# A mixture-of-experts kernel on one core: where TensorE takes the transposes of outputs and of the next rows

## The chip, the core and the metric

The kernel runs on one core of a Trainium2 chip. TensorE (PE) multiplies and transposes, VectorE (DVE) and ScalarE (ACT) compute on tiles, GpSimd (POOL) and SyncE (SP) mainly issue DMAs here. The metric is the device time of one launch in microseconds, the median of the runs of a kernel. Each engine takes its own instructions in the order in which they stand in the program; semaphores make them wait for each other.

## What is computed

`x` is (4, 1024, 1024) in float32. First a cross attention adds to every token a softmax over its normalized similarities with 1024 context vectors. Then follows a mixture of experts, which takes nearly all of the time:

```python
router_probs = jax.nn.softmax(x_flat @ gate_w, axis=-1)
topk_w, topk_idx = jax.lax.top_k(router_probs, 2)          # of 8 experts
topk_w = topk_w / jnp.sum(topk_w, axis=-1, keepdims=True)
...
h = jax.lax.ragged_dot(x_rep_sort, w1, group_sizes)         # 1024 -> 3584
h = jax.nn.silu(h) * jax.lax.ragged_dot(x_rep_sort, w3, group_sizes)
out_sort = jax.lax.ragged_dot(h, w2, group_sizes)           # 3584 -> 1024
...
out = jnp.einsum('tkd,tk->td', out_rep, topk_w)
```

The layer's input is the normalized token, and `out` is added to the token.

## The kernel before

**Before the experts.** The first 550 us compute the attention and the routing, write the tokens to the output and their normalized rows to `h_d`, and fill a table of slots: for each expert, which tokens it has and with which weight.

**Runs and blocks.** The experts' work is a loop over runs on the chip (L841). A run is one expert with up to three blocks of `width` tokens (176 matmul columns for half of a block of 352); a switch picks the code for the number of blocks and the width (L845, `RUNS`). In the profiled execution there are 8 runs of 3 blocks, 24 blocks in all, with half widths of 164, 168, 176 and 180. TensorE's instructions stand in the order in which the code names them (`manual_schedule(engines={ENG.PE})`, L846); the other engines' orders are made by the framework's scheduler from the dependencies.

**A block**, `run` (L745), has two stages. Products are made by a scheme of seven products in place of eight (p1 to p7, Strassen and Winograd's): VectorE makes sums of each weight tile (`weight_sums`, L580, four instructions L585 to L588) and of the tokens (`token_factors`, L709), PE multiplies, and `combine` (L610) puts the results together from four PSUM banks.
- Stage one, i2 = 0 to 13: a tile of w1 and one of w3, each 1 MB in float32, for each of them 28 products in 56 PE instructions (L776), then silu and the product of both, into `g`.
- Stage two, quarters q = 0 to 3 of the output's columns: four tiles of w2, of 8, 8, 6 and 6 slices (`W2K`), that is 4, 4, 3 and 3 values of i2, each of which is a pair of chunks: 7 products in 14 PE instructions (L815). Then `combine` makes `y`, the quarter's result, still transposed. `y` is a single buffer.

**What is transposed.** A finished `y` has to be turned so that tokens lie in the partitions: `tokens_out` (L721) takes 3 groups, each of two 128-wide transposes on PE (L726) into a PSUM tile of the pool `pst`, and VectorE multiplies by the token's weight and adds to `acc` (L728), which holds the tokens' values gathered from the output. After the last quarter GpSimd scatters `acc` back (L733). The rows of the next block, gathered from `h_d` by GpSimd (L650), have to be turned the other way: `tokens_in` (L693) takes 6 groups of four transposes (L699) into `pst`, evicted to `x` by ScalarE (L707, even groups) and VectorE (L705, odd groups) in turn. `pst` has two buffers for both kinds. After the rows, `token_factors` makes the next block's factors, or, in a run's last block, `weight_sums` the sums of the next run's first tile, `w1a`.

**Where they stand.** The list `late` holds what is to be transposed. In stage two it is emptied in one go after the first weight tile of a quarter (L822), so the outputs of quarter q stand after the first tile of quarter q + 1; those of the last quarter stand in the next block's stage one after the first w1 tile (L784), or, between runs, after the next run's first tile (`leftover`, L742, through `y1` and `ids1`). `tokens_in` stands right after the second quarter (L831).

**Weights.** SyncE loads the weight tiles into three buffers (`wp`, L553), each as soon as PE has done with the tile three before.

Of the kernel before, what the change touches and what calls it, by code (L numbers as in the profile page):

```python
# [9 lines left out]
F32 = mybir.dt.float32  # L10
# [8 lines left out]
P = 128  # L19
N = 512  # L20
# [13 lines left out]
def kernel(  # L34
# [14 lines left out]
    nc = tc.nc  # L49
# [4 lines left out]
    KD = D // P  # L54
# [10 lines left out]
    DQ = 4  # L65
# [15 lines left out]
    ident = const.tile([P, P], F32, name="ident")  # L81
# [9 lines left out]
    with ExitStack() as st:  # L91
# [67 lines left out]
        for c in range(KC):  # L159
            pt = ps_t.tile([P, 4, P], F32, tag="pt", name="pt_w")  # L160
# [367 lines left out]
    with ExitStack() as st:  # L528
# [6 lines left out]
        pst = st.enter_context(tc.tile_pool(name="pst", bufs=2, space=PSUM))  # L535
# [5 lines left out]
        RT = 3  # L541
        HK = KD // 2
# [37 lines left out]
        def weight_sums(t, kn, halves, s=None):  # L580
            if s is None:
                s = wp.tile([P, 3, HK, P], F32, tag="s", name="ws")
            f = factors(t, kn, halves, s)
            a11, a12, a21, a22 = f["p1"], f["p2"], f["p7"], f["p4"]
            nc.vector.tensor_tensor(f["p5"], a21, a22, ALU.add)  # L585
            nc.vector.tensor_tensor(f["p6"], f["p5"], a11, ALU.subtract)  # L586
            nc.vector.tensor_tensor(f["p3"], a12, f["p6"], ALU.subtract)  # L587
            nc.vector.tensor_tensor(a21, a11, a21, ALU.subtract)  # L588
            return f
# [70 lines left out]
        rows = [fst.tile([P, D], F32, name=f"rows{s}") for s in range(RT)]  # L660
# [31 lines left out]

        def tokens_in():  # L693

            for s in range(RT):
                for h in range(2):
                    pt = pst.tile([P, N], F32, tag="pt", name="pt_h")
                    for k in range(HK):
                        nc.tensor.transpose(  # L699
                            pt[:, ts(k, P)], rows[s][:, ts(HK * h + k, P)], ident  # L700
                        )
                    src = pt.rearrange("p (a b) -> p a b", b=P)
                    dst = x[:, ds(HK * h, HK), ts(s, P)]
                    if h % 2:
                        nc.vector.tensor_copy(dst, src)  # L705
                    else:
                        nc.scalar.copy(dst, src)  # L707

        def token_factors(n):  # L709

# [8 lines left out]
            return dict(p1=b11, p2=b21, p3=b22, p4=t4, p5=t1, p6=t2, p7=t3)  # L719

        def tokens_out(ids, split, q, y):  # L721
            yv = y.rearrange("p (d c) -> p d c", d=2)
            for s, r in enumerate(split):
                pt = pst.tile([P, N], F32, tag="pt", name="pt_y")
                for d in range(2):
                    nc.tensor.transpose(pt[:r, ts(d, P)], yv[:, d, ds(s * P, r)], ident)  # L726
                part = acc[s][:r, ts(q, QW)]
                nc.vector.scalar_tensor_tensor(  # L728
                    part, pt[:r, :QW], ids.bitcast(F32)[:r, s, 1:2], part, ALU.mult, ALU.add
                )  # L730
            if q == DQ - 1:
                for s, r in enumerate(split):
                    nc.gpsimd.indirect_dma_start(  # L733
                        out=of,
                        out_offset=bass.IndirectOffsetOnAxis(ap=ids[:r, s, 0:1], axis=0),
                        in_=acc[s][:r, :],
                        in_offset=None,
                        bounds_check=T - 1,
                        oob_is_err=False,
                    )  # L740

        def leftover():  # L742
            tokens_out(ids1, [P] * RT, DQ - 1, y1)

        def run(i, ex, s0, blocks, width):  # L745
            n = width // 2
            split = [min(P, width - c) for c in range(0, width, P)]

            def take_ids():
                ids = ip.tile([P, RT, IDW], I32, tag="ids", name="ids")  # L750
                nc.vector.tensor_copy(ids, ids0)
                rd = ip.tile([P, RT], I32, tag="rd", name="rd")
                nc.vector.tensor_copy(rd, rd0)
                return ids, rd

            late = [leftover]
            right = token_factors(n)
            for b in range(blocks):
                ids, rd = take_ids()
                last = b == blocks - 1  # L760
                if not last:
                    load_rows(s0 + (b + 1) * width)
                g = hp.tile([P, NI, 7, n], F32, tag="g", name="g")
                for i2 in range(NI):
                    cs = []
                    for wf, wa, tag in ((w1f, w1a, "c1"), (w3f, w3a, "c3")):
                        t = load(wf, ex, 0, KD, i2 * QW) if b or i2 else wa
                        if t is w1a:
                            left = factors(w1a, KD, False, s1a)
                        else:  # L770
                            left = weight_sums(t, KD, False)
                        pp = banks()
                        for p in ORDER if b or i2 else EARLY:
                            bk, half = BANK[p]
                            for k in range(HK):
                                nc.tensor.matmul(  # L776
                                    pp[bk][:, ts(half, n)], left[p][:, k, :],
                                    right[p][:, k, :],
                                    start=(k == 0), stop=(k == HK - 1),
                                )  # L780
                        c = gp.tile([P, 4 * n], F32, tag=tag, name=tag)
                        combine(pp, n, c, 2 * n)
                        cs.append(c)
                        while late:  # L784
                            late.pop(0)()
                    c1, c3 = cs
                    nc.scalar.activation(c1, c1, AF.Silu)  # L787
                    nc.vector.tensor_tensor(
                        g[:, i2, B11 : B22 + 1, :].rearrange("p a b -> p (a b)"), c1, c3,
                        ALU.mult,  # L790
                    )
                    token_sums(g[:, i2, :, :], n)

                if last:
                    load_first(i + 1)
                    beyond = ip.tile([P, RT], F32, tag="beyond", name="beyond")
                    nc.vector.tensor_scalar(
                        beyond, at, float(width), float(NONE), ALU.is_ge, ALU.mult
                    )
                    nc.vector.tensor_tensor(ids1[:, :, 0], beyond, ids[:, :, 0], ALU.add)  # L800
                    nc.vector.tensor_copy(ids1[:, :, 1], ids[:, :, 1])
                for s, r in enumerate(split):
                    gather(acc[s][:r, :], of, rd, s, r)
                for q in range(DQ):
                    pp = banks()
                    i2 = 0
                    for kn in W2K:
                        t = load(w2f, ex, 2 * i2, kn, q * QW)
                        left = weight_sums(t, kn, True)
                        for k in range(kn // 2):  # L810
                            for p in ORDER:
                                bk, half = BANK[p]


                                nc.tensor.matmul(  # L815
                                    pp[bk][:, ts(half, n)], left[p][:, k, :],
                                    g[:, i2, RIGHT[p], :],
                                    start=(i2 == 0 and half == 0),
                                    stop=(i2 == NI - 1 and p in ENDS),
                                )  # L820
                            i2 += 1
                        while late:  # L822
                            late.pop(0)()
                    if last and q == DQ - 1:
                        combine(pp, n, y1, XW)
                        break
                    y = gp.tile([P, 2 * XW], F32, tag="y", name="y", bufs=1)
                    combine(pp, n, y, XW)
                    late.append(lambda a=ids, d=q, e=y: tokens_out(a, split, d, e))
                    if q == 1:  # L830
                        tokens_in()  # L831
                        if last:
                            weight_sums(w1a, KD, False, s1a)
                        else:
                            right = token_factors(n)

        load_first(0)
        tokens_in()
        weight_sums(w1a, KD, False, s1a)
        n_run = nc.values_load(run_n, min_val=1, max_val=NRUN)  # L840
        with tc.For_i(0, n_run) as i:  # L841
# [3 lines left out]
            for k in tc.Switch(kind, len(RUNS)):  # L845
                with tc.manual_schedule(engines={ENG.PE}):  # L846
                    run(i, ex, s0, *RUNS[k])
        leftover()


# [26 lines left out]
```

## Time and profile before

| | us |
|---|---|
| median of 3 runs | 9158.44 (9154.5 to 9159.08) |
| the profiled execution's own time | 9149.25 |
| its span, first to last instruction | 9147.6 |
| before the loop over runs | about 550 |
| one block, stage one and two (width 352) | about 361 |

The profile is of one execution. Busy time of PE is the union of its matmuls' durations, which overlap, since they are pipelined; PEld are the weight loads, which run beside them. A line such as `L726 PE MATMUL pt_y<-ident,y` names the line of the kernel, the engine, the operation, and what it writes and reads. The largest groups are the products:

```profile
L776 PE MATMUL ps<-x,wt 128*128 128x168 f32 (+3 forms) x15744 | 2510.5, 309 | 0.0
L815 PE MATMUL ps<-g,wt 128*128 128x168 f32 (+3 forms) x10752 | 2027.1, 309 | 0.0
```

After the bar stand the busy time in us and the mean duration of one in ns, then the idle time just before. In a timeline, each row is a start, a duration and what ran, merged where instructions follow each other, with the idle time before it and its cause in brackets.

### The profile page before, as it was taken

To read this page: it belongs to the slowest core of one execution; us is meant where nothing else is said; L and a number is where in the kernel's file an instruction comes from. 1 tells how busy PE (TensorE), PEld (TensorE's weight loads), DVE (VectorE), ACT (ScalarE), POOL (GpSimd) and SP (SyncE) were. 2 spreads that over 40 slices of the span, in tenths; PEclk is the share of its full clock that TensorE was granted. 3 is DMA by queue.
4 is the path that set the end of the run, shared out by engine and by line. 5 is a ranking of instruction groups with operands and counts; after the bars stand their busy time and mean duration, and the time that the engine had idled before them with its cause. 6 is when DMAs were issued, how large, how long until landed. Compare 5 with 4: busy or idle time off the path is not lost. (4 is left out here: it accounts for less than half of the span.)

```text
span 9147.6 us, 139985 instructions
## 1 busy us (share of the span) xinstructions
PE 8852.5 (97%) x59458; PEld 8654.2 (95%) x59459; DVE 5120.9 (56%) x10062; ACT 697.9 (8%) x1527; POOL 409.4 (4%) x503
## 2 busy tenths in 40 slices
PE   8969999999999999999999999999999999999999
PEld 5569999999999999999999999999999999999999
DVE  5655655655645555556546556465565565555554
ACT  3310000000000000000000000000000000000000
POOL 2310000000000000000000000000000000000000
PEclk9979999999999999999999999999999999999999
DMA  3234444443433434344434434434443444434343
GB/s 132 110 120 140 142 143 142 137 146 129 158 128 120 143 130 140 127 139 137 142 129 144 140 119 141 141 129 148 141 147 127 131 137 133 139 129 140 125 137 124
DMA packets 1117374, 1236.39 MB, mean 135 GB/s; under 512 B 35552, under 2 KB 1077984, under 8 KB 1116576
## 3 DMA queue, kind: packets, MB, share of 16 engines
q1 hardware_dynamic: 1079424, 1114.54, 37.2%
q0 software_dynamic: 32656, 107.24, 3.3%
q8 instruction: 501, 8.21, 0.4%
q10 hardware_dynamic: 4496, 3.97, 0.1%
q14 instruction: 297, 2.43, 0.1%
HBM read 1155.26 MB, written 73.53 MB: 134 GB/s over the span
## 5 line engine op out<-in xcount | busy, mean ns | idle before, releaser
L776 PE MATMUL ps<-x,wt 128*128 128x168 f32 (+3 forms) x15744 | 2510.5, 309 | 0.0
L776 PEld LDWEIGHTS ps<-x,wt 128*128 128x128 f32 x15744 | 2353.5, 190 | 0.0
L815 PE MATMUL ps<-g,wt 128*128 128x168 f32 (+3 forms) x10752 | 2027.1, 309 | 0.0
L585 DVE TENSOR_TENSOR ws<-wt 128x512 f32<-128x512 f32 (+1 forms) x1040 | 693.0, 666 | 2077.1 <-DMA wt<-in_L_ffn_w_dram 2021.0
L815 PEld LDWEIGHTS ps<-g,wt 128*128 128x128 f32 x10752 | 1688.8, 190 | 0.0
L776 PE MATMUL ps<-xs,ws 128*128 128x168 f32 (+3 forms) x10624 | 1659.2, 309 | 0.0
L815 PE MATMUL ps<-g,ws 128*128 128x168 f32 (+3 forms) x8064 | 1615.4, 309 | 0.0
L776 PEld LDWEIGHTS ps<-xs,ws 128*128 128x128 f32 x10624 | 1579.1, 190 | 0.0
L815 PEld LDWEIGHTS ps<-g,ws 128*128 128x128 f32 x8064 | 1294.7, 190 | 0.3 <-DVE y L620 0.2
L620 DVE TENSOR_TENSOR c<-ps,p1s 128x352 f32<-128x352 f32 (+3 forms) x672 | 345.9, 515 | 1103.0 <-PE ps L776 1075.0
L776 PE MATMUL ps<-x,ws 128*128 128x168 f32 (+3 forms) x5312 | 883.2, 309 | 0.0
L776 PE MATMUL ps<-xs,wt 128*128 128x168 f32 (+3 forms) x5248 | 872.6, 309 | 0.0
L776 PEld LDWEIGHTS ps<-x,ws 128*128 128x128 f32 x5312 | 804.1, 190 | 0.0
L776 PEld LDWEIGHTS ps<-xs,wt 128*128 128x128 f32 x5248 | 794.4, 190 | 0.0
L586 DVE TENSOR_TENSOR ws<-ws,wt 128x512 f32<-128x512 f32 (+1 forms) x1040 | 692.2, 666 | 30.2
L587 DVE TENSOR_TENSOR ws<-wt,ws 128x512 f32<-128x512 f32 (+1 forms) x1040 | 682.8, 657 | 0.0
L588 DVE TENSOR_TENSOR wt<-wt 128x512 f32<-128x512 f32 (+1 forms) x1040 | 682.5, 656 | 0.0
L619 ACT COPY p1s<-ps 128x168 f32<-128x168 f32 (+3 forms) x768 | 227.8, 297 | 5286.9 <-PE ps L815 2830.1
L787 ACT ACTIVATE c<-c 128x672 f32<-128x672 f32 (+3 forms) x336 | 260.9, 777 | 2559.0 <-DVE c L624 2504.9
L624 DVE TENSOR_TENSOR c<-ps,vu 128x352 f32<-128x352 f32 (+3 forms) x672 | 343.1, 511 | 84.1 <-PE ps L776 80.4
L622 DVE TENSOR_TENSOR vu<-ps,c 128x352 f32<-128x352 f32 (+3 forms) x672 | 341.5, 508 | 6.5 <-PE ps L776 6.2
L650 POOL DMA_INDIRECT rows<-h_d,rd x75 | 82.8, 1104 | 5037.6 <-issue 2487.4
(186 smaller groups left out, 3690.3 us busy)
## 6 DMA issues: line engine op xcount, KB each, us to landing
wt<-in_L_ffn_w_dram SPq DMA_DIRECT2D x848, 1024.0 KB, 4.9
wt<-in_L_ffn_w_dram SPq DMA_DIRECT2D x192, 768.0 KB, 4.6
xt<-in_x_dram SPq DMA_DIRECT2D x32, 512.0 KB, 4.4
out_dram<-x SPq DMA_DIRECT2D x32, 512.0 KB, 2.9
h_d<-hn SPq DMA_DIRECT2D x32, 512.0 KB, 2.6
w1a<-in_L_ffn_w_dram SPq DMA_DIRECT2D x9, 1024.0 KB
w3a<-in_L_ffn_w_dram SPq DMA_DIRECT2D x9, 1024.0 KB, 12.8
cx<-in_ctx_dram SPq DMA_DIRECT2D x4, 1024.0 KB, 8.1
```

Of the source, the lines that this page charges most:

```text
L585: nc.vector.tensor_tensor(f["p5"], a21, a22, ALU.add)
L586: nc.vector.tensor_tensor(f["p6"], f["p5"], a11, ALU.subtract)
L587: nc.vector.tensor_tensor(f["p3"], a12, f["p6"], ALU.subtract)
L588: nc.vector.tensor_tensor(a21, a11, a21, ALU.subtract)
L619: nc.scalar.copy(p1s, pp[0][:, :n])
L620: nc.vector.tensor_tensor(pair(c), pair(pp[1]), twice(p1s), ALU.add)
L622: nc.vector.tensor_tensor(vu, pair(pp[2]), twice(c[:, n : 2 * n]), ALU.add)
L624: nc.vector.tensor_tensor(mid, pair(pp[3]), vu, ALU.add)
L650: nc.gpsimd.indirect_dma_start(out=dst, out_offset=None, in_=src, in_offset=bass.IndirectOffsetOnAxis(ap=rd[:n, s : s + 1], axis=0),)
L776: nc.tensor.matmul(pp[bk][:, ts(half, n)], left[p][:, k, :], right[p][:, k, :], start=(k == 0), stop=(k == HK - 1),)
L787: nc.scalar.activation(c1, c1, AF.Silu)
L815: nc.tensor.matmul(pp[bk][:, ts(half, n)], left[p][:, k, :], g[:, i2, RIGHT[p], :], start=(i2 == 0 and half == 0), stop=(i2 == NI - 1 and ...
```

## The change

The transposes stay as they are, group by group. `tokens_in` and `tokens_out` no longer emit their groups, but return a list of steps, one for each group: 6 for rows, 3 for outputs; the scatter of `acc` becomes a part of its own output step. The steps go into `late`, the rows' behind the outputs of the second quarter, and behind them one step more, `sums`, for the token factors or the sums of `w1a`. From `late` one step is taken at a time: in stage one after each weight tile, in stage two after each pair of chunks but a quarter's first. So a quarter's outputs stand after its successor's pairs 2, 3 and 4; the rows stand in the third quarter after pairs 5 to 10, and `sums` after pair 11; the outputs of the last quarter stand after the first three weight tiles of what follows.

```diff
         def tokens_in():
-            for s in range(RT):
-                for h in range(2):
-                    pt = pst.tile([P, N], F32, tag="pt", name="pt_h")
...
+            def step(s, h):
+                pt = pst.tile([P, N], F32, tag="pt", name="pt_h")
...
+            return [lambda s=s, h=h: step(s, h) for s in range(RT) for h in range(2)]
...
         def tokens_out(ids, split, q, y):
             yv = y.rearrange("p (d c) -> p d c", d=2)
-            for s, r in enumerate(split):
+            def step(s, r):
                 pt = pst.tile([P, N], F32, tag="pt", name="pt_y")
...
-            if q == DQ - 1:
-                for s, r in enumerate(split):
+                if q == DQ - 1:
                     nc.gpsimd.indirect_dma_start(
...
+            return [lambda s=s, r=r: step(s, r) for s, r in enumerate(split)]
...
-            late = [leftover]
+            late = leftover()
...
                         cs.append(c)
-                        while late:
+                        if late:
                             late.pop(0)()
...
                             i2 += 1
-                        while late:
-                            late.pop(0)()
+                            if late and i2 > 1:
+                                late.pop(0)()
...
-                    late.append(lambda a=ids, d=q, e=y: tokens_out(a, split, d, e))
+                    late += tokens_out(ids, split, q, y)
                     if q == 1:
-                        tokens_in()
-                        if last:
-                            weight_sums(w1a, KD, False, s1a)
-                        else:
-                            right = token_factors(n)
+                        late += tokens_in()
+
+                        def sums():
+                            nonlocal right
+                            if last:
+                                weight_sums(w1a, KD, False, s1a)
+                            else:
+                                right = token_factors(n)
+
+                        late.append(sums)
```

More of the change, by code (lines that the diff above doesn't have):

```diff
@@ L693, in tokens_in @@
         def tokens_in():
-            for s in range(RT):
-                for h in range(2):
-                    pt = pst.tile([P, N], F32, tag="pt", name="pt_h")
[L698 to L705, printed above, removed]
-                    else:
-                        nc.scalar.copy(dst, src)
+            def step(s, h):
+                pt = pst.tile([P, N], F32, tag="pt", name="pt_h")
+                for k in range(HK):
+                    nc.tensor.transpose(
+                        pt[:, ts(k, P)], rows[s][:, ts(HK * h + k, P)], ident
+                    )
+                src = pt.rearrange("p (a b) -> p a b", b=P)
+                dst = x[:, ds(HK * h, HK), ts(s, P)]
+                if h % 2:
+                    nc.vector.tensor_copy(dst, src)
+                else:
+                    nc.scalar.copy(dst, src)
+            return [lambda s=s, h=h: step(s, h) for s in range(RT) for h in range(2)]
         def token_factors(n):
@@ L740, in tokens_out @@
                     )
+            return [lambda s=s, r=r: step(s, r) for s, r in enumerate(split)]
         def leftover():
-            tokens_out(ids1, [P] * RT, DQ - 1, y1)
+            return tokens_out(ids1, [P] * RT, DQ - 1, y1)
         def run(i, ex, s0, blocks, width):
@@ L828, in run @@
                     combine(pp, n, y, XW)
-                    late.append(lambda a=ids, d=q, e=y: tokens_out(a, split, d, e))
+                    late += tokens_out(ids, split, q, y)
                     if q == 1:
-                        tokens_in()
-                        if last:
-                            weight_sums(w1a, KD, False, s1a)
-                        else:
-                            right = token_factors(n)
+                        late += tokens_in()
[3 more added lines that the diff above has]
+                                weight_sums(w1a, KD, False, s1a)
+                            else:
+                                right = token_factors(n)
+                        late.append(sums)
         load_first(0)
-        tokens_in()
+        for step in tokens_in():
+            step()
         weight_sums(w1a, KD, False, s1a)
@@ L847 @@
                     run(i, ex, s0, *RUNS[k])
-        leftover()
+        for step in leftover():
+            step()
 _INS = [
```

## The prediction

> **What bounds the kernel now.** I read the busy table first: TensorE is in use over the whole span and no other engine is near it.
>
> ```profile
> PE 8852.5 (97%) x59458; PEld 8654.2 (95%) x59459; DVE 5120.9 (56%) x10062; ACT 697.9 (8%) x1527; POOL 409.4 (4%) x503
> ```
>
> So the time is the length of PE's own queue: what shortens that queue shortens the kernel, if nothing else then becomes late. Next, who PE waits for. Two of the four longest entries lie at the transposes that the change moves, L726 (outputs) and L699 (rows), and they are put down to the evictions of their PSUM tiles:
>
> ```profile
> PE pt_h L699 <- DMA w3a<-in_L_ffn_w_dram: 51.5, 1, 51.5
> PE pt_y L726 <- DVE acc L728: 48.2, 97, 1.9
> PE ps L776 <- issue: 36.6, 4, 10.5
> PE pt_h L699 <- ACT x L707: 30.1, 60, 0.7
> ...
> PE pt_h L699 <- DVE x L705: 2.0, 7, 0.3
> ```
>
> (us in total, times, longest.) The 51.5 us is the one wait before the loop over runs; that part isn't touched. 48.2 + 30.1 + 2.0 = 80 us, but this is a lower end: a wait counts only from the modelled end of the transpose before it (272 ns after its start), while in a steady row the next would have started after 0.11 us. So I look at start to start in the timeline, at one set of rows and one set of outputs:
>
> ```profile
> 8703.58 0.46 PE L815 MATMUL ps<-g,wt 128*128 128x176 f32 x2
> 8703.88 1.04 PE L699 MATMUL pt_h<-ident,rows 128*128 128x128 f32 x8
> 8705.15 0.66 PE L699 MATMUL pt_h<-ident,rows 128*128 128x128 f32 x4 [0.24 <-ACT x L707]
> 8706.48 1.25 PE L699 MATMUL pt_h<-ident,rows 128*128 128x128 f32 x8 [0.68 <-ACT x L707]
> 8708.41 0.66 PE L699 MATMUL pt_h<-ident,rows 128*128 128x128 f32 x4 [0.68 <-ACT x L707]
> 8708.90 0.76 PE L815 MATMUL ps<-g,wt 128*128 128x176 f32 x4
> ```
>
> ```profile
> 8681.77 0.60 PE L726 MATMUL pt_y<-ident,y 128*128 128x128 f32 x4
> 8682.19 1.48 DVE L728 SCALAR_TENSOR_TENSOR acc<-pt_y,ids,acc 128x256 f32<-128x256 f32 x3 [0.51 <-PE pt_y L726]
> 8682.73 0.17 PEld L726 LDWEIGHTS pt_y<-ident,y 128*96 128x96 f32 x2 [0.60 <-DVE acc L728]
> 8682.73 0.42 PE L726 MATMUL pt_y<-ident,y 128*96 128x128 f32 x2 [0.36 <-DVE acc L728]
> ...
> 8682.99 0.76 PE L815 MATMUL ps<-g,wt 128*128 128x176 f32 x4
> ```
>
> The first 8 row transposes take 1.04 us to their last end, so (1.04 - 0.27) / 7 = 0.11 us each; there are two PSUM buffers (pst), so the third group stands still until the first is evicted, and so on. Outputs: four go at once, the third pair waits until VectorE has evicted the first (8682.19 + 0.49).
>
> **The sum.** The trace holds 24 blocks (8 runs of three). From all start times: 24 stretches of 24 row transposes at L699, and 96 of 6 output transposes at L726. First transpose to next matmul, less 0.109 us for each transpose, leaves standing time:
> - rows: 50.7 us, 2.1 us per block;
> - outputs between the tiles of the second product (quarters 0 to 2): 72 stretches, 40.8 us, 0.57 us each;
> - outputs of quarter 3, after the next block's first w1 tile: 24 stretches, 26.2 us; mostly 0.9 us, since VectorE has the combination of that tile in front.
>
> In all 117.7 us of 9149, 4.9 us a block. The chain of waits confirms that this lies on the path: the evictions are its links between stretches of matmuls.
>
> **What the change does, part by part.** *Transposes.* Their number is the same: per block 24 + 4 x 6 = 48, at 0.109 us 5.2 us. They are a piece of PE's queue wherever they stand. What changes is that a group (2 for outputs, 4 for rows) is followed by a 14-matmul pair of chunks (14 x 0.149 = 2.09 us at width 352) or a whole tile of 56 (8.36 us). A buffer is needed again two groups later, 4.2 us at the least, where an eviction takes 0.49 to 0.68 us. All 117.7 us can go if no eviction is later than that.
>
> *More changes of kind.* Stretches of transposes per block go from 5 to 18. What does one cost? In the start times the entry is the matmul's usual pitch (8703.58, two matmuls at 0.149, 8703.88) and the exit is 0.109 plus 0.002 us. 13 more at 0.002 us, over 24 blocks: 0.6 to 0.9 us. Here a rule of the Trainium skill speaks against the change: TensorE: Matmul & The Clock Gate, Part 4: PE-mode transpose, puts a transpose at about 275 ns in a kernel's context, most of it access latency. The profile's duration, 272 ns, is the same; but the pitch is 0.109 us, since successors start under it. If each of the 13 new stretches showed that latency once (0.164 us), it would cost 13 x 0.164 x 24 = 51 us, and the gain be 66; the 120 exits in this trace show none of it, though they all come after rows of 6 or 24. I take 0.9 us. The same section says that transposes do not count as activity for the clock, which would speak for breaking up a row of 5 us; the granted clock in the window 8703 to 8710 is 1.00, so there is nothing to win here (0.80 in the window 8034 to 8060, at a change of runs, is what a throttled stretch looks like).
>
> *VectorE's order.* Evictions on VectorE stand in a fixed order behind weight sums that wait for weights. The built program shows the order of the third quarter, the tightest: sums of the third weight tile around the output evictions, then L585, L586 and L588 of the fourth tile, then the copies of the row groups (0,1) and (1,1), then the first token factor, then the next quarter's first tile with the copy of (2,1). From the quarter's start T, PE asks:
>
> - output groups after chunk pairs 2, 3, 4: T + 4.2 to T + 8.8. The third needs the first's buffer, evicted right after L585 of the third tile, which starts at T + 4.5 to 6.6 in quarters 0, 1 and 3 of this trace: evicted by about T + 7.7.
> - row groups after pairs 5 to 10, ScalarE and VectorE by turns; so the VectorE ones always take the same buffer. (1,1), after pair 8, comes at 8 x 2.09 + 3 x 0.22 + 3 x 0.44 = T + 18.7 and needs the copy of (0,1). That stands behind L585 of the fourth tile, which starts at T + 12.4 to 13.75 in every quarter of this trace. It shifts by 0.4 us, as two output groups now lie in front of the end of the first tile; so about T + 14, then 0.56 + 0.56 + 0.55 + 0.68: done near T + 16.3. Slack some 2.4 us.
> - (2,1), after pair 10, needs the copy of (1,1), written under pair 9. No weights are in front of it. It fits.
>
> Where the cover goes, PE stands still for what is missing. y has one buffer: combined by about T + 2.5, first read at T + 4.2, last at T + 8.8, written again from T + 30.
>
> *Token factors and sums of w1a* are asked for after pair 11 of the third quarter, 23 us later than before, and needed some 35 us on. The sums of w1a keep their place in VectorE's order; the factors run in the third quarter's last third, where the trace has VectorE waiting for weights. 0 us. *Scatters* (GpSimd) leave after their own output group, two tiles later for the last; read back only by the next gather, over 200 us later. 0. SP's and GpSimd's orders are unchanged; the next row gather needs the rows read, 23 us later, and has 200 us. 0.
>
> *What is late next.* With 4.9 us less per block of 360, PE asks for weights 1.4% faster. A 1 MB tile lands 4.9 us after issue, per 8.36 us tile, and the sums of the fourth tile end near T + 16 for use at about T + 26. Nothing.
>
> 9149.25 - (117.7 - 0.9) = 9032.4 us for the profiled execution; its time is 9.2 us under the median of the runs, so the median becomes 9158.44 - 116.8 = **9042 us**.
>
> **Rivals.**
> - *Part of the waits stays*, as changes of kind cost more than the long rows show, or evictions are now and then late. For: no group of 2 or 4 between dense matmuls with both edges is in this trace. Against: edges of 0.002 us. With 51 us lost, 9093; with a quarter of the waits back, 9071. Chance 0.14.
> - *Weights or another engine fill the gap*, and the time stays: VectorE is at 56% and its idle time ends on weights (2021 us in L585's row), so they could be late once PE runs ahead. Against: 8 to 10 us of slack. 9150 to 9158. Chance 0.03.
> - *Slower: PE, strictly in order, stands before the row group (1,1)* because its buffer's eviction is behind a weight sum that waits for a DMA. In the trace before, the sums ahead of an eviction always had their weights by then. It starts when the fourth tile's L585 is 2.4 us later than estimated, and outweighs the gain when it is 2.4 + 4.9 = 7.3 us later in every block, at T + 21. With 10 us late, 24 x (10 - 2.4 - 4.9) = +65: 9223. The trace has no start later than T + 13.75 in 96 quarters. Chance 0.05.
> - *The change doesn't do what it says*: the built program has the groups between the pairs on PE. No chance given.
>
> **How the numbers follow.** Likeliest 0.78: 9042, give or take 9, about what one execution and the median differ by. The low end is 9033. The high end goes into the partly hidden case, up to a quarter of the waits, 9072. A measurement here can tell about 0.2%, 18 us; so faster 0.92 (the first case and the first rival), same 0.03, slower 0.05.
>
> **What would show it.** Right: waits of L726 and L699's line in the loop (now L730) on L732, L705 and L707 nearly gone; transposes in x2 and x4 between x14 matmuls, 0.109 us pitch; PE's busy time slightly changed, span near 9032. Wrong: a wait on DVE x L705 of microseconds (the slower rival); intervals of 0.2 us or more at the edges (first rival); new waits of the products' matmuls (now L781 and L820) on weight sums (second).

## The result and the profile after

The changed kernel takes 9035.69 us (9034.8 to 9036.42), the kernel before 9158.76 us in the same series: a ratio of 0.9864, 95% interval 0.9851 to 0.9876. Predicted were 9042 us, within 9033 to 9072. The profiled execution takes 9036.42 us against 9149.25, 112.8 us less; 116.8 were predicted.

The busy table, then PE's waits (us in total, times, longest) at the lines of the transposes:

```profile
PE 8818.7 (98%) x59458; PEld 8659.7 (96%) x59459; DVE 5115.4 (57%) x10062; ACT 698.7 (8%) x1527; POOL 423.7 (5%) x503
```

```profile
PE pt_h L699 <- DMA w3a<-in_L_ffn_w_dram: 51.5, 1, 51.5
...
PE pt_y L730 <- issue: 1.3, 1, 1.3
PE pt_y L730 <- DVE acc L732: 0.8, 1, 0.8
...
PE pt_h L699 <- DVE x L705: 0.2, 1, 0.2
```

The instructions are as many as before. What is left of waits at L730 and L699 is the one before the loop and the one after it; the 48.2, 30.1 and 2.0 us are gone. PE's busy time is 33.8 us less although it does the same: each wait began under the tail of a transpose, which counted as busy.

The chain of waits of one block (start, us, what) shows the new order, which is PE's alone:

```profile
8605.80 2.09 PE ps L820 x14
8607.89 0.22 PE pt_y L730 x2
8608.11 2.09 PE ps L820 x14
8610.20 0.44 PE pt_h L699 x4
8610.64 2.09 PE ps L820 x14
8612.73 0.44 PE pt_h L699 x4
...
8622.84 0.44 PE pt_h L699 x4
8623.28 12.53 PE ps L820 x84
```

A pair of chunks is 2.09 us, an output group 2 x 0.109 us, a row group 4 x 0.109. Before, the same chain had ScalarE and VectorE as links between the transposes, as here at one set of rows:

```profile
8704.51 0.59 ACT x L707
8705.15 0.67 PE pt_h L699 x4
8705.84 0.59 ACT x L707
8706.48 1.26 PE pt_h L699 x8
```

In the timeline of the changed kernel the edges are seen start to start:

```profile
8609.74 0.46 PE L820 MATMUL ps<-g,wt 128*128 128x176 f32 x2
8610.04 0.60 PE L699 MATMUL pt_h<-ident,rows 128*128 128x128 f32 x4
8610.48 0.76 PE L820 MATMUL ps<-g,wt 128*128 128x176 f32 x4
```

Two matmuls take 0.30 us, as between matmuls alone, and four transposes 0.44. From all start times the standing time, counted as in the prediction, is 0.2 us, of 117.7.

| start to start, us, inside the loop over runs | before | after |
|---|---|---|
| first to last PE instruction | 8583.2 | 8469.0 |
| standing at transposes | 117.7 | 0.2 |
| of these: rows / outputs in stage two / in stage one | 50.7 / 40.8 / 26.2 | 0.1 / 0.1 / 0.0 |
| the seven changes of run | 75.6 | 75.7 |

(The loop here begins with the last transposes before it.) 114.2 us are gained there; the stage before it was 1.0 us longer in this execution, and the end behind PE's last instruction 0.4 us.

### The profile page after: what moved, and what is told of

The parts are those of the page before. It is cut to its first block, busy times and chain, and to the rows that moved or that the text cites. A ratio compares the mean times of both kernels' runs of the same rounds, so it can differ in the third digit from the quotient of the medians.

```text
span 9034.7 us, 139994 instructions
## 1 busy us (share of the span) xinstructions
PE 8818.7 (98%) x59458; PEld 8659.7 (96%) x59459; DVE 5115.4 (57%) x10062; ACT 698.7 (8%) x1527; POOL 423.7 (5%) x503
## 5 line engine op out<-in xcount | busy, mean ns | idle before, releaser
L820 PE MATMUL ps<-g,wt 128*128 128x168 f32 (+3 forms) x10752 | 2071.0, 309 | 0.0
L585 DVE TENSOR_TENSOR ws<-wt 128x512 f32<-128x512 f32 (+1 forms) x1040 | 693.7, 667 | 1991.4 <-DMA wt<-in_L_ffn_w_dram 1948.6
```

The lines of the kernel that those rows point to most:

```text
L820: nc.tensor.matmul(pp[bk][:, ts(half, n)], left[p][:, k, :], g[:, i2, RIGHT[p], :], start=(i2 == 0 and half == 0), stop=(i2 == NI - 1 and ...
```

## The experiments

My theory: in a row of groups, PE, strictly in order, finds both PSUM buffers of the transposes taken from the third group on and stands for an eviction, so the gain is the standing time and no more. The rivals: it is VectorE's combination ahead of the evictions, that is the place, that makes the wait; it is the number of buffers as such; or a part of the gain has another cause. (A row of groups with more than two buffers was not run.)

### The same kernel again

No edit.

> The changed kernel once more, for the size of its gain. If the gain is the standing time of PE at the transposes and nothing else (117.7 us in the trace of before, 0.2 us in that of after), the median lies 113 to 118 us under the kernel before. The first comparison of medians gave 123 us; if something else is gained too that the trace does not show as standing time, it is 120 us or more again.

9033.77 us (9027.33 to 9034.48) against 9161.15: a ratio of 0.9862 (0.9847 to 0.9877), by the medians 127 us. The profiled execution takes 9034.48 us, with 0.2 us of standing time. That is the expected sign of something more than 118 us, so I followed it below.

### One part alone: rows, or outputs

Rows one at a time, outputs in a row (`in_a_row` takes all steps of a list at once):

```diff
-            late = leftover()
+            late = [lambda: in_a_row(leftover())]
...
-                            if late and i2 > 1:
+                            if late and i2 > 3:
...
-                    late += tokens_out(ids, split, q, y)
+                    late.append(lambda o=tokens_out(ids, split, q, y): in_a_row(o))
```

> Rows one group at a time, outputs in a row after a quarter's fourth pair of chunks (the end of its first weight tile) as before. Theory (PE stands for the third and later group of a row, which finds both PSUM buffers taken): the 50.7 us at the rows go, the 66.9 us at the outputs stay: 50 us faster than before, about 9108. Rival (most is gained where VectorE has the combination in front, that is at the outputs of the last quarter, and rows in a row cost little, since ScalarE takes half of them): 20 us or less.

Outputs one at a time, rows in a row:

```diff
-                        late += tokens_in()
+                        in_a_row(tokens_in())
...
-                        late.append(sums)
+                        sums()
```

> Outputs one group at a time, rows in a row right after the second quarter as before. Theory: 66.9 us faster than before (40.8 in stage two, 26.2 in stage one), about 9092; with the rows-only kernel the two gains add up to that of the whole change. Rival (the parts overlap: once PE no longer stands at the one, VectorE is later for the other): the two gains sum to clearly more or less than 117 us, by 15 us or more.

Rows only: 9104.51 us, a ratio of 0.9942 (0.9929 to 0.9956). Outputs only: 9080.96, a ratio of 0.9915 (0.9902 to 0.9929). PE's waits, rows only, then outputs only:

```profile
PE pt_y L730 <- DVE acc L732: 51.5, 97, 2.4
...
PE pt_h L699 <- DVE x L705: 0.2, 1, 0.2
```

```profile
PE pt_h L699 <- ACT x L707: 30.1, 60, 0.7
PE pt_h L699 <- DVE x L705: 2.6, 9, 0.4
...
PE pt_y L730 <- DVE acc L732: 0.8, 1, 0.8
```

Each part takes its own wait away and leaves the other's nearly where it was: 70.4 us of standing time stay in the first (66.9 at the outputs before), 51.7 in the second (50.7 at the rows before). In the loop the profiles gain 44.0 and 65.2 us, together 109.2, the whole change 114.2. So the parts add up to within 5 us, and neither rival holds. By the medians each kernel of this series gains 12 to 15 us more than its profile does in the loop, the whole change too.

### Place without granularity

Rows in one row still, but after the third quarter's seventh pair of chunks; outputs in a row as before:

```diff
-                        late += tokens_in()
+                        late.append(lambda: in_a_row(tokens_in()))
...
-                            if late and i2 > 1:
+                            if late and i2 in (4, 7, 11):
```

(The outputs' edits are those of the rows-only kernel.)

> The place of the rows without the granularity: outputs in a row as before, rows in one row too, but after the third quarter's seventh pair of chunks in place of right before that quarter, where VectorE is busy with the combination. Theory (two buffers and a row of six groups make the wait, wherever the row stands): rows stand for 1.5 to 2.1 us per block as before, outputs as before: within 15 us of the kernel before, 9144 to 9159. Rival (the wait comes from VectorE's combination in front of the copies, so the new place is what gains): the 50 us of the rows go, about 9108.

9128.77 us, a ratio of 0.9973 (0.9962 to 0.9984): by the medians 28 us faster than before, between both expectations. The rows' standing time is 27.3 us, of 50.7. The timeline of one such row (width 328):

```profile
851.19 0.44 PE L824 MATMUL ps<-g,wt 128*128 128x164 f32 x2
851.47 1.04 PE L699 MATMUL pt_h<-ident,rows 128*128 128x128 f32 x8
852.75 2.64 PE L699 MATMUL pt_h<-ident,rows 128*128 128x128 f32 x16 [0.24 <-ACT x L707]
855.23 0.72 PE L824 MATMUL ps<-g,wt 128*128 128x164 f32 x4
```

24 x 0.109 are 2.62 us, and the row takes 3.76: 1.14 us of standing, where it was 2.1. So my theory was half right for the rows: the wait that two buffers make, when VectorE is free, is 1.14 us a block; 0.98 us more went with the old place. There VectorE has `combine` and weight sums ahead of its copies, in the row of before that the prediction shows:

```profile
8705.66 0.52 DVE L624 TENSOR_TENSOR y<-ps,vu 128x352 f32<-128x352 f32 x1
8706.10 0.33 DVE L625 TENSOR_TENSOR y<-ps,vu 128x176 f32<-128x176 f32 x1
8706.35 0.68 DVE L705 COPY x<-pt_h 128x512 f32<-128x512 f32 x1
```

The second group was transposed by 8704.9 and is copied only from 8706.35 to 8707.03. Yet the fourth group starts at 8706.48, as soon as ScalarE has copied the third (8705.84 + 0.58). So at the old place the groups do not take the two buffers in turn: the fourth uses the one that the third has just left. In the trace of before its transposes wait for ScalarE's semaphore in all 24 rows, in the kernel with the new place for VectorE's. That is why the table of waits names ScalarE for the rows although VectorE is the late one. How the 0.98 us divide between VectorE's lateness and the other order of buffers is not shown. One group at a time avoids all of it.

### How many at a time

In stage two, two steps after every second pair, and three after pairs 4, 8 and 12:

```diff
-                            if late and i2 > 1:
-                                late.pop(0)()
+                            for _ in range(2):
+                                if late and i2 % 2 == 0:
+                                    late.pop(0)()
```

```diff
-                            if late and i2 > 1:
-                                late.pop(0)()
+                            for _ in range(3):
+                                if late and i2 in (4, 8, 12, 13):
+                                    late.pop(0)()
```

> In stage two, two groups at once after every second pair of chunks; stage one as in the changed kernel. Theory (two groups find two buffers, 4.2 us later both are free again): nearly no standing time, under 0.5 us per block, so within 12 us of the changed kernel. Rival (each group must be alone between matmuls): half of the stage two waits, 1.3 us per block, 30 us or more slower than the changed kernel.

> In stage two, three groups at once after pairs 4, 8 and 12; stage one as in the changed kernel. Theory: the third of each three stands until the first is evicted: outputs 0.57 us in three quarters as before, rows twice 0.4 to 0.6 us, so 2.5 to 2.9 us per block, 60 to 70 us slower than the changed kernel. Rival (spreading the groups over the quarter is enough, whatever their number at once): within 15 us of the changed kernel.

Two: 9033.89 us, a ratio of 0.9864 (0.9849 to 0.9879), as the changed kernel; 0.2 us of standing time. Three: 9095.59, 0.9932 (0.9919 to 0.9946), 62 us slower than two in the same series. PE's waits with three:

```profile
PE pt_y L730 <- DVE acc L732: 26.8, 73, 0.8
PE pt_h L699 <- DVE x L705: 8.5, 25, 0.3
PE pt_h L699 <- ACT x L707: 5.7, 24, 0.2
```

Of 73 waits 72 are one in each quarter's outputs, as before; the 24 on ScalarE and 24 on VectorE are one in each row of three. Standing time 65.2 us: 40.5 at outputs, 24.7 at rows. So it is the third group at once that waits; single groups are not needed, two at once are as good.

### One buffer

```diff
-        pst = st.enter_context(tc.tile_pool(name="pst", bufs=2, space=PSUM))
+        pst = st.enter_context(tc.tile_pool(name="pst", bufs=1, space=PSUM))
```

> The changed kernel with one PSUM buffer for the transposes in place of two. Theory (what counts is that the eviction before is over when a group starts, and groups are 2.1 us or more apart): of nine groups in stage two only the row group (1,0) finds its buffer taken, asked for near T + 16.1 us of the third quarter and set free near T + 16.3, by a copy behind the weight sums of the fourth tile: 0.2 to 0.5 us per block, 5 to 12 us in all, about 9042 to 9050. Rival (it is the number of buffers that matters: each group would wait for the eviction of the one before, 0.5 to 0.9 us for each of 18 groups a block): 150 us and more over the changed kernel, slower than before.

9040.19 us, 0.9869 (0.9854 to 0.9884). PE's waits:

```profile
PE pt_y L730 <- DVE acc L732: 4.0, 8, 1.0
PE pt_h L699 <- DVE x L705: 2.1, 4, 0.8
PE pt_h L699 <- ACT x L707: 2.1, 3, 0.7
```

That is a handful of waits, where 432 groups now share one buffer. In the start times 12 of them lie in the loop, 5.5 us; the others lie before and after it, where the groups are still in a row. The kernel is 6.4 us slower than the changed kernel of the same series, in the expected 5 to 12 us; the place came only in part as expected: I had given one row group of every block, it was 5 row groups and 7 output groups, in some blocks only. The rival's 150 us are excluded. What counts is the time between a group and the one that wants its buffer.

### Ten us more than the standing time

By the medians the kernels gain some 10 us more than the standing time. First, the kernel before twice more, unchanged, for its profile:

> The kernel before, unchanged, for a second profile: its runs spread over 20 us and the first profiled execution lies near the fast end of them, while those of the changed kernel lie within 10 us. If the standing time at the transposes itself varies, this profile shows it away from 117.7 us, by as much as the execution is away from 9149 us. If the stage before the loop or the changes of runs vary, the standing time is 117 to 119 us again.

> The same once more: a third profile of the kernel before, with the same two answers.

The two executions took 9148.79 and 9139.25 us, with 119.0 and 117.5 us of standing time: it hardly varies, the rest does, and the traces show where. In the profiles of all runs PE's first transposes of rows, just before the loop, start 538.7 to 552.7 us after the span's start, whatever the order in the loop. From there to PE's last instruction it takes 8582.8 to 8588.0 us in five executions with the order of before and 8468.6 to 8469.0 in three of the changed kernel, which is 114 to 119 us apart. So most of the spread lies in the stage before the loop, which the change leaves as it was.

Then the kernel before timed against itself, and the changed functions with every step at the old place, the same instructions in the same order on every engine as before:

```diff
-                        late += tokens_in()
+                        in_a_row(tokens_in())
...
-                            if late and i2 > 1:
+                            if late and i2 == 4:
```

(with the outputs' edits of the rows-only kernel, and `sums()` at once.)

> The kernel before, timed against itself. All variants so far, whatever they change, gain 9 to 14 us more by their medians than their profiled executions gain against the profiled one of before; the change's own 123 to 127 us against 114 in the loop are of this kind. If that is an uncertainty of the comparison (in a series of runs the kernel before comes out 10 us high), the ratio here is 0.999, 10 us under itself. If not, it is 1.000 within 4 us, and the variants share a gain that the standing time doesn't show.

> The changed kernel's functions (lists of steps, the scatter inside the step), with all steps taken in a row and at the places of before; every engine has the same instructions in the same order as before. If the 10 us that all variants share come with the new code, this gains 10 us with 117 to 119 us of standing time left. If they are of the comparison, it does as the kernel before does against itself, within 5 us. If the standing time is all, no gain in the profile: its execution within 10 us of 9149.

Before against itself: 9145.32 us against 9149.92, a ratio of 0.9998 (0.9988 to 1.0007). Written anew: 9147.92, 1.0 (0.9991 to 1.0009), with 119.3 us of standing time. So the new code by itself gains nothing, and a comparison does not by itself put the kernel before 10 us too high. But in this series, on another chip, it lay 7 to 11 us lower than in the series with the variants.

> The changed kernel a third time. Timed against itself and against its own order written anew, the kernel before came out at 9145 to 9150 us, and not at 9157 to 9161 as in the series with the variants. If the gain is the standing time alone, it is 114 to 118 us in a series in which the kernel before is near 9148, and the changed kernel stays at 9032 to 9036. If the difference is one of the two chips, which moves both kernels alike, the changed kernel comes down with it, to about 9022 to 9026, and the gain stays 123 to 127.

9028.03 us (9021.5 to 9034.17) against 9146.58, a ratio of 0.9867 (0.985 to 0.9883): 119 us. Of both expectations half came true: the changed kernel came down by 6 us, no more than its own four runs differ, and the gain is near the standing time. The chip as such is not the cause: this series and the one with the place-only, two-at-a-time and three-at-a-time kernels ran on the chip of the same number, and the kernel before took 9146.58 us in the one and 9157.12 in the other. The last few us of the gain stay open, as no execution of 9157 us or more was profiled: the three series give 123, 127 and 119 us by their medians, the profiled executions 113, and series of one and the same kernel differ by 10 us. All three intervals contain 0.9872, which is 117 us.

## Why the prediction was right

- *The standing time at the transposes, 117.7 us, is on PE's path and can go.* Right: 0.2 us are left, and the loop is 114.2 us shorter. Counting start to start was the step that carried it; the table of waits alone would have given 80 us. Rows and outputs each lost their own wait when changed alone.
- *Changes of kind cost 0.002 us each.* Right for groups of 2 and 4 too: 0.109 us per transpose, the entry at the matmul's own pitch, 0.002 us at the exit. The 275 ns of the Trainium skill (TensorE: Matmul & The Clock Gate, Part 4: PE-mode transpose) are given there in a passage on bf16; the float32 transposes here have a duration of 272 ns in the profile, and between dense matmuls they take 109 ns each from start to start. A price of 0.164 us for each new stretch would have cost 51 us, and the trace has none of it.
- *The slack.* T is the start of the third quarter's first product, and row group (0,1) is the second of the six. Its copy was put near T + 16.3 us, behind the fourth tile's L585 near T + 14, and wanted at T + 18.7. Over 24 blocks L585 starts at T + 13.5 (12.9 to 13.9), the copy ends at T + 15.7 (15.1 to 16.1), and PE asks at T + 18.3 (17.6 to 19.1). The slower rival needed the copy 2.4 us later than that; in no block was it late, the least slack being 2.2 us, and with one buffer only, where the slack is 2.5 us less, waits for evictions appear, with 5.5 us in all.
- *Next late: nothing.* Right. L585's idle time that ends on weights, summed over the span, falls from 2021.0 to 1948.6 us and does not vanish, so VectorE still waits for weights that PE doesn't yet need. The rival in which weights fill the gap is excluded.
- *9032.4 us for the profiled execution*: it took 4.0 us more. 1.0 lies before the loop and 0.4 behind it. In the loop 2.3 are longer pitches of the products just after the changes of run, where the granted clock is 0.50 for some microseconds (window 7946.4 to 7950.4 of the changed kernel). This is not shown to be chance: in the 60 us after each start of a run the pitches are longer than usual by 21.3 to 21.8 us in all in three executions of the changed kernel, by 18.4 to 19.3 us in five with the order of before; the other kernels lie between 17.9 and 22.7 us, with no order that I can name. The sum had no term for it, and its cause stays open. The edges, at 0.0025 us, took 0.8 us, which the sum had.
- *9042 us for the median*: 6 us too high. The sum took over from the kernel before that the median lies 9.2 us above the profiled execution; in the changed kernel it lies 0.7 us below. This miss of 9.9 us and the 4.0 us above go opposite ways, so that 9042 came within 6 us is in part luck.
- What I had not seen: all of the reason for the rows' wait. I named the two buffers, and read the timeline as if every group waited for the one two before it. The buffers are 1.14 us of 2.1 a block; the rest was the place, next to `combine`, where the fourth group waits for the third. It made no difference to the sum, since the change removed both.

## What to carry to other kernels

Here a short burst of transposes among dense matmuls, on an engine that works in order, cost next to nothing beyond its own 109 ns for each (0.0025 us a burst); what cost was that a burst was longer than its buffers. Take at most as many groups at once as there are buffers and leave an eviction's time, with what stands ahead of it on its engine, before the next. To know what a wait is worth, count from start to start: the modelled tail of a pipelined instruction hides a part of the standing time in the table of waits, here 37 of 117.7 us.

## What was unexpected

The 18 groups of a block, spaced, can share one PSUM buffer nearly for nothing (5.5 us in the loop, of 8470), so the second buffer's 2 KB per partition could be used for something else in this order. And series of runs of the unchanged kernel differ by more than 10 us (medians of 9146.58 to 9161.15 us in series of several runs), 0.16%, close to the 0.2% that I took as what a measurement tells; the ratios of the changed kernel within its series, 0.9862 to 0.9867, agree far better.
